# A gated graph network and an attention layer: gates r and z from seven block products, and LayerNorm's last pass on ScalarE

## The chip, the cores and the metric

The kernel runs on one core of a Trainium2 chip. Its time is the device time of one execution in microseconds (us). A core has a matrix engine (TensorE: PE for matmuls, PEld for the loads of their stationary operand), VectorE (DVE), ScalarE (ACT), GpSimd (POOL) and a queue engine (SP), each with an instruction stream of its own. Matmul results land in PSUM (8 banks of 512 fp32 columns on 128 partitions), which DVE and ACT read; everything else is held in SBUF.

## What is computed

64 graphs of 256 nodes with 256 features, an adjacency matrix for each. Layer 0 is a gated graph network with three rounds, layer 1 a graph attention with four heads; both take a normalised input and add to the residual stream.

```python
def _gru_cell(inp, h, w_ih, w_hh, b_ih, b_hh):
    gi = inp @ w_ih.T + b_ih
    gh = h @ w_hh.T + b_hh
    i_r, i_z, i_n = jnp.split(gi, 3, axis=-1)
    h_r, h_z, h_n = jnp.split(gh, 3, axis=-1)
    r = sigmoid(i_r + h_r); z = sigmoid(i_z + h_z)
    n = tanh(i_n + r * h_n)
    return (1.0 - z) * n + z * h

h = maximum(layernorm(x), 0)                      # layer 0
g = h
for i in range(3):
    m = einsum('bnd,de->bne', g, weight[i])
    g = _gru_cell(einsum('bst,bsd->btd', (adj != 0), m), g, w_ih, w_hh, b_ih, b_hh)
x = x + g
h = maximum(layernorm(x), 0)                      # layer 1
v = (h @ W.T + b) in 4 heads of 64
p = softmax over j of where(adj == 1, leaky_relu(l_src[i] + l_dst[j], 0.2), -9e15)
out = x + sum_j p[i, j] v[j]
```

## The kernel before

All arithmetic is fp32 (gather multiplies fp32r parts). Two graphs make a pair (32 pairs); a pair's 512 nodes are the 512 columns of a transposed tile `hT` with 256 features in two blocks of 128 partitions. At the start the message weights are multiplied into the input weights once, so a round is: `gather` (sum of the neighbours' states, exact adjacency times a state split into two parts `hi` and `lo`), then for each of two feature blocks four gates `hn`, `r`, `z`, `in` (line 288). A gate is one PSUM tile of 128 x 512 from the pool `ps_g` (four banks); r and z sum over four products (two blocks of `hT`, two of `aggr`), hn and in over two. A matmul in fp32 appears as two MATMUL instructions in the trace, called passes here. ACT and DVE then form r, z, n and the new state: tanh for the sigmoids (L302, L311), L303 and L306 for r times hn, L314 and L316 for n, a difference on POOL (L319), L320 and L323 for the state.

The order of work on PE is written by hand. `todo` holds pieces by slot and place; a slot has eight places, one gate each, and a slot is one round of one pair. Pair p has its rounds in slots 3p, 3p+2 and 3p+4, so that rounds of neighbouring pairs alternate and every slot is filled. The other pieces hang between the gates: `load` (SP), `prepare` (LayerNorm of x and the masks from adj), `turn` (transposes of the normalised rows), `split` (back to rows, hi and lo, from round 2 on), `gather`; for layer 1, `residual` (adds x, LayerNorm), `turn1`, `values`, `spread` (a row of scores through HBM to all partitions, `rows`), `score` (L375 to L387: masked scores, their maximum, exponentials and sums), `turn2`, `mix`, `finish`. The pattern repeats every three slots, one pair's whole work. Slots 1 (mod 3) hold two scores, slots 2 two more and the residual, slots 0 values and spread.

PE keeps the written order. On the other engines the order is made at build time from what is ready first in a planned time, earlier pieces first among those; on the chip each engine keeps that order and waits at the first instruction whose inputs are missing.

LayerNorm (`normalise`, L193) takes statistics per row on DVE (L198, L199), the power -1/2 on POOL (L202) and four DVE passes of 128 x 256 for (x - m) times the factor (L205). The ReLU follows where the rows are used: in the copy after the transposes (L215), in hi (L251) and lo (L252).

Of the kernel before, what the change touches and what calls it, by code (L numbers as in the profile page):

```python
# [17 lines left out]
P = 128  # L18
# [8 lines left out]
def gated_gnn_then_gat_kernel(  # L27
# [46 lines left out]
    ps_g = ctx.enter_context(tc.tile_pool(name="ps_g", bufs=4, space=bass.MemoryType.PSUM))  # L74
    ps_m = ctx.enter_context(tc.tile_pool(name="ps_m", bufs=4, space=bass.MemoryType.PSUM))

    def bank(name):
        return ps_m.tile([P, 512], F32, tag="mm", name=name)
# [6 lines left out]
    def load_first():  # L85
        xt = io.tile([P, R, D], F32, tag="x", name="x_0", bufs=4)
        nc.sync.dma_start(xt, x_rows[:T, :].rearrange("(r q) d -> q r d", q=P))
        at = io.tile([P, R, N], I32, tag="adj", name="adj_0", bufs=1)
        nc.sync.dma_start(at, adj_rows[:T, :].rearrange("(r q) t -> q r t", q=P))
        return xt, at  # L90
# [90 lines left out]

    setup_scope.close()
# [10 lines left out]
    def normalise(src, name):  # L193

        st = small.tile([P, R, 6], F32, tag="st", name=f"st_{name}")
        mv = small.tile([P, R, 2], F32, tag="mv", name=f"mv_{name}")
        for r in range(R):
            nc.vector.bn_stats(st[:, r, :], src[:, r, :])  # L198
            nc.vector.bn_aggr(mv[:, r, :], st[:, r, :])  # L199
        rstd = small.tile([P, R], F32, tag="rstd", name=f"rstd_{name}")  # L200
        nc.vector.tensor_scalar_add(rstd, mv[:, :, 1], EPS)
        nc.gpsimd.tensor_tensor(rstd, rstd, mhalf, ALU.pow)  # L202
        xn = sb.tile([P, R, D], F32, tag="xn", name=f"xn_{name}")
        for r in range(R):
            nc.vector.tensor_scalar(  # L205
                xn[:, r, :], src[:, r, :], mv[:, r, 0:1], rstd[:, r : r + 1], op0=ALU.subtract, op1=ALU.mult
            )
        return xn

    def relu_T(xn, dst, k, name):  # L210

        pt = bank(f"pt_{name}_{k}")
        for r in range(R):
            nc.tensor.transpose(pt[:, ts(r, P)], xn[:, r, ts(k, P)], ident)
        nc.scalar.activation(dst[:, k, :], pt, AF.Relu)  # L215

    def halves(name):
        hi = sb.tile([P, R, D], F32R, tag="hi", name=f"hi_{name}")
        lo = sb.tile([P, R, D], F32R, tag="lo", name=f"lo_{name}")
        return hi, lo  # L220

# [10 lines left out]
    class Pair:  # L232


        def __init__(self, p):
            self.p = p
            self.rden, self.pr, self.prT, self.oT = {}, {}, {}, {}

        def load(self):
            p = self.p  # L240
            self.xt = io.tile([P, R, D], F32, tag="x", name=f"x_{p}", bufs=4)
            nc.sync.dma_start(self.xt, x_rows[ts(p, T), :].rearrange("(r q) d -> q r d", q=P))
            self.at = io.tile([P, R, N], I32, tag="adj", name=f"adj_{p}", bufs=1)
            nc.sync.dma_start(self.at, adj_rows[ts(p, T), :].rearrange("(r q) t -> q r t", q=P))


        def prepare(self):
            p = self.p
            self.xn = normalise(self.xt, f"a{p}")
            self.hi, self.lo = halves(f"a{p}")  # L250
            nc.scalar.activation(flat(self.hi), flat(self.xn), AF.Relu)  # L251
            nc.vector.scalar_tensor_tensor(  # L252
                flat(self.lo), flat(self.xn), 0.0, flat(self.hi), op0=ALU.max, op1=ALU.subtract
            )
# [5 lines left out]
        def turn(self, k):  # L260
            if k == 0:
                self.hT = sb.tile([P, KD, T], F32, tag="hT", name=f"hT_{self.p}", bufs=5)
            relu_T(self.xn, self.hT, k, f"a{self.p}")

        def split(self, l):
            n_ = f"{self.p}_{l}"
            self.hi, self.lo = halves(n_)
            for i in range(PB):
                pt = natural(self.hT, i, n_)
                rows = batch_rows(i)  # L270
                nc.scalar.copy(flat(self.hi, rows), pt)
                nc.vector.tensor_sub(flat(self.lo, rows), pt, flat(self.hi, rows))

        def gather(self, l):
            n_ = f"{self.p}_{l}"
            self.aggr = sb.tile([P, KD, T], F32, tag="aggr", name=f"aggr_{n_}")
            for e in range(KD):
# [8 lines left out]
                nc.scalar.copy(self.aggr[:, e, :], pt)  # L286

        def gate(self, l, c, kind):

            n_ = f"{self.p}_{l}_{c}"  # L290
            hh, ih = wT["hh"], w_in[:, l]
            g = {"r": c, "z": KD + c, "hn": 2 * KD + c, "in": 2 * KD + c}[kind]
            pt = ps_g.tile([P, T], F32, tag="g", name=f"p{kind}_{n_}")
            parts = [(hh, self.hT, k) for k in range(KD)] if kind != "in" else []
            parts += [(ih, self.aggr, k) for k in range(KD)] if kind != "hn" else []
            for j, (w, src, k) in enumerate(parts):
                nc.tensor.matmul(pt, w[:, k, ts(g, P)], src[:, k, :], start=(j == 0), stop=(j == len(parts) - 1))  # L297
            if kind == "hn":
                self.p_hn = pt
            elif kind == "r":  # L300
                r_ = sb.tile([P, T], F32, tag="r", name=f"r_{n_}")
                nc.scalar.activation(r_, pt, AF.Tanh, bias=brz[:, g : g + 1], scale=0.5)  # L302
                nc.vector.tensor_scalar(r_, r_, 0.5, 0.5, op0=ALU.mult, op1=ALU.add)  # L303
                self.t_ = sb.tile([P, T], F32, tag="t", name=f"t_{n_}")
                g_n = 2 * KD + c
                nc.vector.scalar_tensor_tensor(  # L306
                    self.t_, self.p_hn, bh[:, g_n : g_n + 1], r_, op0=ALU.add, op1=ALU.mult
                )
            elif kind == "z":
                self.z_ = sb.tile([P, T], F32, tag="z", name=f"z_{n_}")  # L310
                nc.scalar.activation(self.z_, pt, AF.Tanh, bias=brz[:, g : g + 1], scale=0.5)  # L311
            else:
                t_, z_ = self.t_, self.z_
                nc.vector.tensor_add(t_, pt, t_)  # L314
                y_ = sb.tile([P, T], F32, tag="n", name=f"n_{n_}")
                nc.scalar.activation(y_, t_, AF.Tanh, bias=bi[:, g : g + 1])  # L316

                d_ = sb.tile([P, T], F32, tag="d", name=f"d_{n_}")
                nc.gpsimd.tensor_sub(d_, self.hT[:, c, :], y_)  # L319
                nc.vector.scalar_tensor_tensor(d_, z_, 1.0, d_, op0=ALU.add, op1=ALU.mult)  # L320
                if c == 0:
                    self.hT2 = sb.tile([P, KD, T], F32, tag="hT", name=f"hT_{self.p}_{l}", bufs=5)
                nc.vector.scalar_tensor_tensor(self.hT2[:, c, :], d_, 0.5, y_, op0=ALU.mult, op1=ALU.add)  # L323
                if c == KD - 1:
                    self.hT = self.hT2
# [11 lines left out]
        def turn1(self):  # L337
            self.hbT = sb.tile([P, KD, T], F32, tag="hbT", name=f"hbT_{self.p}", bufs=1)
            for k in range(KD):
                relu_T(self.xn, self.hbT, k, f"b{self.p}")  # L340
# [27 lines left out]
        def score(self, i, s):  # L368
# [4 lines left out]
            zz = sb.tile([P, H, N], F32, tag="zz", name=f"zz_{p}_{r}", bufs=3)  # L373
# [16 lines left out]
        def turn2(self, i, s):  # L390
# [3 lines left out]
            for j in range(KN):  # L394
# [4 lines left out]
                if j % 2:  # L399
                    nc.vector.tensor_copy(dst, src)  # L400
                else:
                    nc.scalar.copy(dst, src)

        def mix(self, i):
# [11 lines left out]
            self.oT[i] = sb.tile([P, H // 2, N], F32, tag="oT", name=f"oT_{p}_{i}")  # L416
            nc.scalar.copy(flat(self.oT[i]), po)

        def finish(self, i):
# [7 lines left out]
            o = sb.tile([P, KN, D], F32, tag="o", name=f"o_{p}_{i}")  # L427
# [13 lines left out]
    todo = {}  # L441

    def at(slot, k, piece, *args):
        todo.setdefault(8 * slot + k, []).append((piece, args))

    KINDS = ("hn", "r", "z", "in")
    pairs = [Pair(p) for p in range(NPAIR)]
    pairs[0].xt, pairs[0].at = first
    for q in pairs:
# [3 lines left out]
        at(s0 - 2, 2, q.prepare)  # L453
        at(s0 - 1, 2, q.turn, 0)
        at(s0 - 1, 3, q.turn, 1)
        at(s0 - 1, 6, q.gather, 0)
        for l in range(L):
            s = s0 + 2 * l
            if l:
                at(s - 1, 3, q.split, l)  # L460
                at(s - 1, 6, q.gather, l)
            for k in range(8):
                at(s, k, q.gate, l, k // 4, KINDS[k % 4])
        s += 1
        at(s, 4, q.residual)
        at(s + 1, 1, q.turn1)
        for r in range(R):
            at(s + 1, 3 + r // 2, q.values, r)
        at(s + 1, 6, q.spread)
        for piece, i, j, *place in (  # L470
            (q.score, 0, 0, 2, 1), (q.score, 0, 1, 2, 3), (q.turn2, 0, 0, 2, 6), (q.turn2, 0, 1, 3, 0),
            (q.score, 1, 0, 2, 6), (q.score, 1, 1, 3, 1), (q.turn2, 1, 0, 3, 6), (q.turn2, 1, 1, 4, 0),
        ):
            at(s + place[0], place[1], piece, i, j)
        at(s + 3, 2, q.mix, 0)
        at(s + 3, 4, q.finish, 0)
        at(s + 4, 2, q.mix, 1)
        at(s + 4, 6, q.finish, 1)

    for place in todo.values():  # L480
        place.sort(key=lambda x: x[0].__name__ == "gather")
    for place in todo.values():
        place.sort(key=lambda x: x[0].__name__ == "gate")
# [34 lines left out]
```

## Time and profile before

| | |
|---|---|
| runs, median | 2801.98 us (2799.52 to 2802.9, three) |
| profiled execution, its own time | 2799.7 us |
| its span, first to last instruction | 2797.7 us |
| mean granted TensorE clock | 0.993 |
| gate matmuls, passes of 128 x 512 | 6 groups of x768 |
| transposes, passes of 128 x 128 | x2560 in the steady part |
| gather, passes of 128 x 256 | x1536 |
| HBM traffic | 69.87 MB read, 17.04 MB written |

The span is cut into forty slices of 70 us. Busy tenths of an engine and the granted clock in each:

```profile
PE   7999999999999999999999999999999999999995
DVE  4346666556656556656566656566656566665466
ACT  1224434334433334343333443343443344443343
PEclk9999999999999999999999999999999999999998
```

Matmul records last to the end of their pipeline, so the durations of neighbours overlap; the distance from start to start is the pitch that counts. The costliest groups, with busy time and mean ns of one after the bar:

```profile
L297 PE MATMUL pz<-hT,hh_T 128*128 128x512 f32 x768 | 363.9, 596 | 0.0
L297 PE MATMUL pr<-aggr,w_in 128*128 128x512 f32 x768 | 360.9, 592 | 0.0
L302 ACT ACTIVATE r<-pr,brz 128x512 f32<-128x512 f32 x192 | 131.5, 685 | 526.5 <-PE pr L297 526.3
L379 DVE SCALAR_TENSOR_TENSOR zz<-zz 128x1024 f32<-128x1024 f32 x128 | 155.4, 1214 | 1.1
L400 DVE COPY prT<-ppT 128x512 f32<-128x512 f32 x128 | 87.0, 680 | 1.5 <-PE ppT L397 1.5
L351 DVE TENSOR_TENSOR val<-pv,b_val 128x264 f32<-128x264 f32 x128 | 52.3, 427 | 151.1 <-PE pv L348 151.1
L126 ACT COPY msgT<-pmT 128x256 f32<-128x256 f32 x6 | 1.9, 375 | 11.0 <-PE pmT L125 11.0
```

### The profile page before, as it was taken

Reading aid. Unit: us, or ns where it says so; the run is one execution under the profiler, and the core shown is the slowest. Engines: PE = TensorE matmul, PEld = TensorE weight load, DVE = VectorE, ACT = ScalarE, POOL = GpSimd, SP = SyncE. Lnnn points to the kernel's source line nnn. Section 1 sums busy time; section 2 is a strip of 40 time slices with the busy share of each in tenths; the row PEclk is TensorE's granted clock in tenths of the full one; section 3 lists DMA queues with packets and bytes.
Section 4 is the critical chain, followed back from the end, with each engine's and each line's share of the span. In section 5 each row is a group of like instructions: output and inputs, shape, how many; then the busy total and the mean of one; then the engine's idle time right before and its main releaser. Section 6 shows DMA issues by size and latency. Waiting matters only on the chain. (4 is left out here: it accounts for less than half of the span.)

```text
span 2797.7 us, 28381 instructions
## 1 busy us (share of the span) xinstructions
PE 2744.3 (98%) x10468; PEld 1518.7 (54%) x10468; DVE 1670.1 (60%) x3326; ACT 1053.5 (38%) x2311; POOL 413.6 (15%) x327
## 2 busy tenths in 40 slices
PE   7999999999999999999999999999999999999995
PEld 4455555555555555555555555555555555555553
DVE  4346666556656556656566656566656566665466
ACT  1224434334433334343333443343443344443343
POOL 0011111111111111111111111111111111111111
PEclk9999999999999999999999999999999999999998
DMA  3000110110110100101101101101101101100000
GB/s 92 8 31 12 38 38 27 38 38 12 39 31 34 38 26 24 38 27 38 38 16 34 38 27 38 38 12 38 38 27 39 38 12 38 38 27 23 23 23 31
DMA packets 61451, 88.73 MB, mean 32 GB/s; under 512 B 5248, under 2 KB 57088, under 8 KB 57216
## 3 DMA queue, kind: packets, MB, share of 16 engines
q1 hardware_dynamic: 56064, 84.16, 9.4%
q10 hardware_dynamic: 5248, 2.76, 0.4%
q8 instruction: 82, 1.34, 0.2%
q14 instruction: 57, 0.47, 0.1%
HBM read 69.87 MB, written 17.04 MB: 31 GB/s over the span
## 5 line engine op out<-in xcount | busy, mean ns | idle before, releaser
L319 POOL TENSOR_TENSOR d<-hT,n 128x512 f32<-128x512 f32 x192 | 265.5, 1383 | 1667.5 <-ACT n L316 1667.5
L384 ACT ACTIVATE zz<-zz,nmx 128x256 f32<-128x256 f32 x512 | 254.0, 497 | 292.3 <-DVE nmx L381 292.3
L297 PE MATMUL pz<-hT,hh_T 128*128 128x512 f32 x768 | 363.9, 596 | 0.0
L297 PE MATMUL phn<-hT,hh_T 128*128 128x512 f32 x768 | 362.7, 595 | 0.0
L297 PE MATMUL pin<-aggr,w_in 128*128 128x512 f32 x768 | 361.1, 593 | 0.0
L297 PE MATMUL pr<-hT,hh_T 128*128 128x512 f32 x768 | 361.0, 592 | 0.0
L297 PE MATMUL pz<-aggr,w_in 128*128 128x512 f32 x768 | 360.9, 592 | 0.0
L297 PE MATMUL pr<-aggr,w_in 128*128 128x512 f32 x768 | 360.9, 592 | 0.0
L302 ACT ACTIVATE r<-pr,brz 128x512 f32<-128x512 f32 x192 | 131.5, 685 | 526.5 <-PE pr L297 526.3
L314 DVE TENSOR_TENSOR t<-pin,t 128x512 f32<-128x512 f32 x192 | 131.4, 684 | 324.9 <-PE pin L297 324.8
L320 DVE SCALAR_TENSOR_TENSOR d<-z,d 128x512 f32<-128x512 f32 x192 | 132.6, 691 | 242.2 <-POOL d L319 242.2
L311 ACT ACTIVATE z<-pz,brz 128x512 f32<-128x512 f32 x192 | 130.7, 681 | 384.6 <-PE pz L297 384.6
L375 DVE SCALAR_TENSOR_TENSOR zz<-rows,val,noedge 128x256 f32<-128x256 f32 x512 | 220.9, 480 | 66.0 <-DMA rows<-line 66.0
L297 PEld LDWEIGHTS pz<-aggr,w_in 128*128 128x128 f32 x768 | 146.0, 190 | 183.6 <-issue 183.6
L297 PEld LDWEIGHTS pr<-aggr,w_in 128*128 128x128 f32 x768 | 146.0, 190 | 183.6 <-issue 178.6
L297 PEld LDWEIGHTS pr<-hT,hh_T 128*128 128x128 f32 x768 | 143.7, 190 | 169.3 <-issue 159.3
L297 PEld LDWEIGHTS pin<-aggr,w_in 128*128 128x128 f32 x768 | 138.7, 190 | 139.1 <-issue 137.0
L316 ACT ACTIVATE n<-t,bi 128x512 f32<-128x512 f32 x192 | 138.2, 720 | 187.7 <-DVE t L314 185.4
L297 PEld LDWEIGHTS phn<-hT,hh_T 128*128 128x128 f32 x768 | 139.6, 192 | 127.5 <-issue 121.7
L297 PEld LDWEIGHTS pz<-hT,hh_T 128*128 128x128 f32 x768 | 133.8, 190 | 120.8 <-issue 120.8
L397 PEld LDWEIGHTS ppT<-ident,zz 128*128 128x128 f32 x1024 | 120.8, 142 | 82.2 <-issue 57.8
L379 DVE SCALAR_TENSOR_TENSOR zz<-zz 128x1024 f32<-128x1024 f32 x128 | 155.4, 1214 | 1.1
(91 smaller groups left out, 3552.8 us busy)
## 6 DMA issues: line engine op xcount, KB each, us to landing
rows<-line SPq DMA_DIRECT2D x32, 1024.0 KB, 6.6
x<-in_x_dram SPq DMA_DIRECT2D x32, 512.0 KB, 4.0
adj<-in_adj_dram SPq DMA_DIRECT2D x32, 512.0 KB, 3.9
out_dram<-o SPq DMA_DIRECT2D x64, 256.0 KB, 2.2
w_msg<-in_L_gnn_weight_dram ACTq DMA_DIRECT2D x1, 768.0 KB
ih_nat<-in_L_gnn_w_ih_dram ACTq DMA_DIRECT2D x1, 768.0 KB
hh_nat<-in_L_gnn_w_hh_dram ACTq DMA_DIRECT2D x1, 768.0 KB
line<-srow SPq DMA_DIRECT2D x32, 8.0 KB
```

What stands on the lines that cost most here:

```text
L297: nc.tensor.matmul(pt, w[:, k, ts(g, P)], src[:, k, :], start=(j == 0), stop=(j == len(parts) - 1))
L302: nc.scalar.activation(r_, pt, AF.Tanh, bias=brz[:, g : g + 1], scale=0.5)
L311: nc.scalar.activation(self.z_, pt, AF.Tanh, bias=brz[:, g : g + 1], scale=0.5)
L314: nc.vector.tensor_add(t_, pt, t_)
L316: nc.scalar.activation(y_, t_, AF.Tanh, bias=bi[:, g : g + 1])
L319: nc.gpsimd.tensor_sub(d_, self.hT[:, c, :], y_)
L320: nc.vector.scalar_tensor_tensor(d_, z_, 1.0, d_, op0=ALU.add, op1=ALU.mult)
L375: nc.vector.scalar_tensor_tensor(zz[:, h, :], self.rows[:, h, ts(i, N)], self.val[:, r, D + h : D + h + 1], self.noedge[:, r, :], op0=ALU. ...
L379: nc.vector.scalar_tensor_tensor(flat(zz), flat(zz), ALPHA, flat(zz), op0=ALU.mult, op1=ALU.max)
L384: nc.scalar.activation(zz[:, h, :], zz[:, h, :], AF.Exp, bias=nmx[:, h : h + 1], accum_out=den[:, h : h + 1])
L397: nc.tensor.transpose(pt[:, ts(h, P)], self.pr[r][:, h, ts(j, P)], ident)
```

## The change

For r and for z the product is a 2 x 2 block matrix (output blocks and feature blocks of 128) times a 2 x 2 block matrix (feature blocks, and the pair's two graphs of 256 columns). Eight block products become seven, from sums of blocks: of the weights, made once at the start (`block_sums`), and of the columns, made in each round (`column_sums`, for hT on POOL, for aggr on DVE). The sums over hh and in run in the same PSUM columns. Two banks serve a gate: half of `px` takes products 1, 6, 7 and 4 one after the other, and is copied out between them (`ab`, `c22`); `pyz` takes 5 and 3 in one half and 2 in the other. hn and in keep their 512 columns, now issued one matmul at a time between the products. A slot has 22 units (`U`). The two PSUM pools of four banks become one of eight.

In LayerNorm ACT makes ReLU(x * rstd - m * rstd) in one pass per row block (`shift` is -m * rstd); the later copies lose their ReLU, round 1's hi and lo move to the slot of `split`. The copies of `prT` all go to ACT. The buffers of x, xn, hi, lo, hT, zz, oT and o shrink, and the places are rewritten in units.

```diff
-    ps_g = ctx.enter_context(tc.tile_pool(name="ps_g", bufs=4, space=bass.MemoryType.PSUM))
-    ps_m = ctx.enter_context(tc.tile_pool(name="ps_m", bufs=4, space=bass.MemoryType.PSUM))
+    ps = ctx.enter_context(tc.tile_pool(name="ps", bufs=8, space=bass.MemoryType.PSUM))
...
+    def block_sums(w, name):
+        out_ = const.tile([P, 4, 2, P], F32, name=f"sums_{name}")
...
+        nc.vector.tensor_add(out_[:, 0], a21, a22)
+        nc.vector.tensor_sub(out_[:, 1], out_[:, 0], a11)
+        nc.vector.tensor_sub(out_[:, 2], a11, a21)
+        nc.vector.tensor_sub(out_[:, 3], a12, out_[:, 1])
+        return out_
...
-            nc.vector.tensor_scalar(
-                xn[:, r, :], src[:, r, :], mv[:, r, 0:1], rstd[:, r : r + 1], op0=ALU.subtract, op1=ALU.mult
+            nc.scalar.activation(
+                xn[:, r, :], src[:, r, :], AF.Relu, bias=shift[:, r : r + 1], scale=rstd[:, r : r + 1]
             )
...
+    def column_sums(src, engine, name):
+        t = sb.tile([P, 4, N], F32, tag=f"sum{name[0]}", name=f"sum_{name}")
+        s_ = src.rearrange("q k (i n) -> q k i n", i=PB)
+        engine.tensor_sub(t[:, 0::2, :], s_[:, :, 1, :], s_[:, 0, :, :])
+        engine.tensor_add(t[:, 1, :], t[:, 2, :], s_[:, 0, 0, :])
+        engine.tensor_sub(t[:, 3, :], s_[:, 1, 0, :], t[:, 1, :])
+        return t
...
+            if l == 0:
+                nc.scalar.copy(flat(self.hi), flat(self.xn))
+                nc.vector.tensor_sub(flat(self.lo), flat(self.xn), flat(self.hi))
+                return
...
+        def product(self, l, kind, m):
...
+            x_, y_, z_ = self.px[:, :N], self.pyz[:, :N], self.pyz[:, N:]
+            out_ = {1: x_, 6: x_, 7: x_, 4: x_, 5: z_, 3: z_, 2: y_}[m]
+            parts = ((wT["hh"], sums_h, self.hT, self.th), (w_in[:, l], sums_in[l], self.aggr, self.ts_))
...
+                nc.tensor.matmul(
+                    out_, lhs, rhs, start=(j == 0 and m in (1, 5, 2)), stop=(j == 1), skip_group_check=True
+                )
...
+            if m == 1:
+                nc.scalar.copy(self.ab[:, 0, :], x_)
+            elif m == 6:
+                nc.scalar.copy(self.ab[:, 1, :], x_)
+            elif m == 5:
+                nc.scalar.copy(self.c22, z_)
+            elif m == 7:
+                nc.vector.tensor_add(self.c22, x_, self.c22)
+                tanh(self.g_[:, 3, :], self.c22, 1)
+            elif m == 2:
+                nc.vector.tensor_add(flat(self.ab), self.pyz, flat(self.ab))
+                tanh(flat(self.g_[:, :2, :]), flat(self.ab), 0)
+                if kind == "r":
+                    self.reset(l, 0)
+            elif m == 4:
+                tanh(self.g_[:, 2, :], x_, 1)
+                if kind == "r":
+                    self.reset(l, 1)
...
-                if j % 2:
-                    nc.vector.tensor_copy(dst, src)
-                else:
-                    nc.scalar.copy(dst, src)
+                nc.scalar.copy(dst, src)
...
+    UNITS = [
+        *("r1 r5 hn00 r6 hn01 r3 hn10 r7 hn11 r2 r4".split()),
+        *("z1 z5 in00 z6 in01 z3 z7 in10 z2 in11 z4".split()),
+    ]
...
+        at(s0 - 2, 5, q.prepare)
+        at(s0 - 1, 5, q.turn, 0)
+        at(s0 - 1, 8, q.turn, 1)
         for l in range(L):
             s = s0 + 2 * l
...
+            at(s - 1, 9, q.split, l)
+            at(s - 1, 10, q.sum_h)
+            at(s - 1, 17, q.gather, l)
...
+            at(s, 20, q.update, l, 0)
+            at(s, 21, q.update, l, 1)
         s += 1
+        at(s, 12, q.residual)
+        at(s + 1, 3, q.turn1)
...
+        at(s + 1, 17, q.spread)
...
+            (q.score, 0, 0, 2, 3), (q.score, 0, 1, 2, 8), (q.turn2, 0, 0, 2, 17), (q.turn2, 0, 1, 3, 0),
+            (q.score, 1, 0, 3, 0), (q.score, 1, 1, 3, 4), (q.turn2, 1, 0, 3, 17), (q.turn2, 1, 1, 4, 0),
```

## The prediction

> **What bounds the kernel now.** First the page's busy times, then the stretches of one steady period, then TensorE's timeline.
>
> ```profile
> PE 2744.3 (98%) x10468; PEld 1518.7 (54%) x10468; DVE 1670.1 (60%) x3326; ACT 1053.5 (38%) x2311; POOL 413.6 (15%) x327
> ```
>
> ```profile
> 90.00:1385.00 1295.00, 1295.00 (x4909) 713.23 (x4908) 770.12 (x1531) 491.71 (x1059) 194.45 (x151) 1.00 0.09 30
> 1385.00:1411.00 26.00, 26.00 (x85) 13.40 (x84) 20.30 (x36) 11.49 (x30) 3.25 (x2) 1.00 0.15 54
> 1411.00:1440.00 29.00, 29.00 (x122) 16.20 (x121) 18.77 (x48) 11.69 (x28) 5.79 (x5) 1.00 0.09 28
> 1440.00:1471.00 31.00, 31.00 (x125) 17.82 (x124) 12.56 (x21) 10.23 (x16) 3.88 (x3) 1.00 0.12 31
> ```
>
> The columns are length, then busy time of PE, PEld, DVE, ACT and POOL. From 90 us on PE is never idle, at the full granted clock. The last three rows are one period of three slots, one pair's work: 86.0 us, 32 of them. DVE is busy 51.6 of the 86 us, but 20.3 of 26 in the first slot. So PE bounds; what follows needs the pitch of its instructions, because its durations overlap.
>
> ```profile
> 1450.20 1.88 PE L297 MATMUL pz<-aggr,w_in 128*128 128x512 f32 x4
> 1451.92 1.94 PE L348 MATMUL pv<-w_val,hbT 128*128 128x264 f32 x8
> 1453.70 1.04 PE L227 MATMUL pn<-ident,hT 128*128 128x128 f32 x8
> ```
>
> Four passes over 512 columns start 1.72 us before what follows them: 430 ns a pass (each fp32 matmul is two passes). Eight passes over 264 columns take 1.78 us: 222.5 ns, or 0.843 ns a column, against 0.840 for 512. A pass of 256 columns should then cost 215 to 222 ns; I take 216. At 264 columns every pass has its own weights too, so a new weight load per narrow pass is already covered by this row.
>
> **The gain.** In each of the 96 slots r and z now take 16 matmuls = 32 wide passes, 32 x 0.430 = 13.76 us. After: 2 gates x 7 products x 2 sources x 2 passes = 56 passes x 0.216 = 12.10 us. Saved 1.66 us a slot, 159 us in all; at 222.5 ns a pass it is 1.30 us and 125 us. hn, in, gather and the transposes keep their passes. I take 158.
>
> [...]
>
> **What the other engines pay, per period.** DVE gains three column sums a slot (one 512 wide like L323, 0.69, two 256 wide like L351's 0.43), two c22 additions (0.43) and two 512-wide additions into ab (0.69): 3.8 us a slot, 11.4; shift 0.3. It loses 8 L205 (0.41 each, 3.3) and 4 L400 (0.68, 2.7). Net +5.7: 57 of about 81 us. ACT gains 18 copies of 256 columns (375 ns in L126, at most L384's 497: I take 0.375, 6.8 us), six tanh more, since each gate's two of 512 columns (0.685, L302) become one and two halves (0.45 each, between 0.375 and 0.5; 1.3), 8 passes of xn (0.4 each, 3.2) and 4 prT copies (0.58, 2.3): +13.6, so 47 of 81. POOL gains three sums a slot: L319's 1.27 us for 512 wide, and 0.64 to 1.27 for each narrow one (I take 0.65): 2.6 a slot, 7.8. None of the three becomes the bound by its sum. Sixteen block sums at the start (0.41 each, 6.6 us of DVE) lie in gaps DVE has while it waits for L131; 2 us are charged for what sticks out and 1 for the tail's prT copies, now on one engine.
>
> Edits I cost at nothing: fewer buffers (x, xn, hi, lo, zz, hT, o, oT). xn has one buffer: prepare's copy is last read by split at unit 9 of slot 2 (mod 3), residual's is written some 6 us after unit 12 and first read at unit 3 of the next slot, thirteen units and 11 us on; if that cover went, PE would wait there for the rest. hi and lo are read by gather eight units after they are written and rewritten a slot later. The x load, issued on SP ahead of adj, now waits for the residual one slot before; it lands in 4.0 us and its first use is over a slot later. If that wait came late by some us on SP, line, rows and out behind it would slip; rows is the one that matters, at 2 us a period.
>
> **Where a stall comes from.** Now a gate's bank is read once, at the end, and four banks rotate. After the change px is written, copied, and added to again, and half of pyz too, so PE waits for ACT or DVE inside a gate. Per slot: r1 to r6, z1 to z6 and z6 to z7 (ACT), and r7 to r4 (DVE), each with two units of 0.86 us = 1.72 between; r5 to r3, r6 to r7, z5 to z3 (ACT) and z7 to z4 (DVE) with three, 2.58. A return trip with a free engine takes the pipeline's end (1.88 - 1.72 = 0.16), a copy (0.375, or 0.43 on DVE) and two signals (0.04 to 0.2): about 0.7. The spare is 1.0 or 1.9 us. Everything behind a waiting matmul on PE waits with it. How promptly are PE's results read today?
>
> ```profile
> 1407.59 1.88 PE L297 MATMUL pz<-aggr,w_in 128*128 128x512 f32 x4
> ```
>
> ```profile
> 1410.11 0.51 ACT L384 ACTIVATE zz<-zz,nmx 128x256 f32<-128x256 f32 x1 [3.45 <-DVE nmx L381]
> ...
> 1412.10 0.67 ACT L311 ACTIVATE z<-pz,brz 128x512 f32<-128x512 f32 x1
> ```
>
> pz is ready at 1409.47. ACT is idle but stands at an exponential that waits for DVE's maximum, then runs four: z starts 2.63 us late. A pin ready at 1411.19 is read by L314 at 1414.63, 3.4 us late, behind scores. Nothing waits for either today. Which waits recur:
>
> ```profile
> ACT zz L384 <- DVE nmx L381: 292.3, 127, 11.0
> DVE d L320 <- POOL d L319: 242.2, 163, 2.2
> DVE zz L375 <- DMA rows<-line: 66.0, 29, 6.6
> ```
>
> ACT stands 2.3 us at each of 4 score rows a period and then is busy 2.0 more. With ACT returns every 4.5 us on average, about one a burst is caught, in a random part of it: a loss of 0 to 1.6 us (2.6 less the spare of 1.0), I take 0.4, as about half the returns have the longer spare. Four give 1.6. In the score slot rows come 2.3 us late (66.0 / 29), which moves the row's ten DVE and ACT instructions and the c22 addition of r7 queued among them: 2.3 less 1.0 is 1.3 at most, 0 at least; I take 0.8. Together 2.4 us a period, 77 us.
>
> POOL's sums lengthen this if they meet DVE:
>
> ```profile
> 1404.04 1.98 POOL L319 TENSOR_TENSOR d<-hT,n 128x512 f32<-128x512 f32 x1 [14.23 <-ACT n L316]
> ```
>
> Alone it takes 1.27; here it starts during L379 (both DVE inputs in SBUF) and ends 0.71 later. [...] DVE has 24 us a period free, so the sum above leaves it out and the range's top has it.
>
> **The sum.** Against the profiled execution: 2799.7 - 158 + 3 + 77 = 2721.7. It stands 2.3 us below the median of 2801.98, inside its runs. I forecast 2722.
>
> **Rivals.** (1) Every return comes in time, PE stays gapless: 2799.7 - 158 + 3 = 2645, at most 2665 with 0.6 us a period. For it: DVE and ACT are under 75% by their sums, and the order on DVE is filled greedily (the xn_a of 1438.9 is for transposes one period after those of 1419.0, 66 us later). Against: the two late reads above lie in an ordinary period. Chance 0.20.
> (2) Slower: returns coupled to the score rows. Each of the 4 bursts catches a return with the short spare (1.6 each, 6.4), and r7 to r4 waits out rows and a POOL meeting (1.3 + 1.3), less the 2 that one stall spares the next: 7 us a period, 224 us: 2869. It decides above (158 - 3) / 32 = 4.8 us a period. For it: DVE busy 20.3 of 26 us in that slot, +3.8 less a third of what leaves it, 2.0, in a slot PE now crosses in some 24; the banks px, pyz and in or hn then fill up too. Against: stalls give DVE and ACT time to catch up, and the slot at 12.56 of 31 us absorbs a lag. With a middling 5 to 6 us the time is 2805 to 2840. Chance 0.24.
> (3) The narrow passes don't give the saving: at 222.5 ns it is 125 us and with the same stalls 2755; it is nil at 246 ns. Against: the 264-column row. Chance 0.06.
> (4) The forecast, some stalls, 1 to 4.4 us a period: 2675 to 2785. Chance 0.50.
>
> The range is 2650 to 2830: about 0.1 is left below, in case 1, and 0.1 above, in case 2. The forecast's own range is 2675 to 2785. Runs of this kernel tell 0.2% (5.6 us) from no change. Faster: 0.20 + 0.48 of case 4 + 0.03 of case 3 = 0.71; within 0.2%: 0.04; slower: 0.25.
>
> **What would show it.** Pass pitch: groups of px and pyz matmuls at 0.86 us a unit where nothing waits; over 0.9 refutes the gain. Stalls: idle time of PE or PEld ahead of the second writes of px and pyz, put down to ACT's ab or c22 copies or DVE's c22 addition, 40 to 130 us in sum, most of it in the slots with scores; if it is under 20, case 1, if over 155, case 2. Idle time ahead of other products, put down to the column sums (r5, z5), would be a wait I have costed at nothing: after gather, six units lie before r5's second half, 5 us against 2.3. A DVE busy time far from 1855 us, ACT from 1490 or POOL from 665 would refute the rows used.

## The result, and the profile after

The changed kernel takes 2872.52 us (median of 4 runs, 2870.39 to 2875.74) beside 2802.23 for the kernel before: ratio 1.0254, 95% interval 1.0236 to 1.0271. It is 70 us slower, and the profiled execution (2872.8) is 228 us above the 2645 that the prediction gave for a TensorE without gaps.

Busy times on the page of the changed kernel, then its own stretches over one period (length; busy time of PE, PEld, DVE, ACT, POOL; granted clock):

```profile
PE 2644.2 (92%) x12772; PEld 1957.0 (68%) x12772; DVE 2022.2 (70%) x3694; ACT 1449.6 (50%) x3463; POOL 695.7 (24%) x615
```

```profile
1407.00:1438.00 31.00, 26.99 (x124) 20.01 (x123) 23.30 (x39) 15.02 (x39) 8.47 (x7) 0.94 0.17 60
1438.00:1467.00 29.00, 29.00 (x152) 21.81 (x151) 23.90 (x46) 15.00 (x39) 8.23 (x7) 1.00 0.09 28
1467.00:1494.30 27.30, 26.04 (x125) 19.09 (x124) 14.93 (x33) 15.09 (x33) 5.00 (x5) 1.00 0.01 2
```

PE, which was never idle in the steady part, now is for 5.3 of 87.3 us, 4.0 of them in the first stretch, and there the clock falls to 0.94. No other engine is a bound by its sum. The waits of PE, with their total, number and longest:

```profile
PE px_z L355 <- ACT ab_z L364: 73.1, 30, 2.5
PE px_r L355 <- DVE c_r L370: 46.4, 30, 1.8
PE px_z L355 <- DVE c_z L370: 36.9, 28, 2.3
...
PE px_r L355 <- ACT ab_r L364: 14.6, 20, 1.7
```

These are z1 to z6, r7 to r4, z7 to z4 and r1 to r6: four returns inside a gate, 171 us. The first three come once in nearly every period, at the same place, and each of these three has its own cause in the timeline (start, duration, engine, instruction; in brackets the idle time before it and what ended it).

**r7 to r4, in the slot with the first two scores.**

```profile
1417.93 4.02 DVE L464 SCALAR_TENSOR_TENSOR zz<-rows,val,noedge 128x256 f32<-128x256 f32 x5
...
1424.54 0.41 DVE L370 TENSOR_TENSOR c_r<-px_r,c_r 128x256 f32<-128x256 f32 x1
...
1418.16 1.38 POOL L244 TENSOR_TENSOR sum_h<-hT 128x512 f32<-128x512 f32 x1 [1.60 <-DVE hT L412]
1419.62 0.79 POOL L245 TENSOR_TENSOR sum_h<-sum_h,hT 128x256 f32<-128x256 f32 x1
1420.48 0.79 POOL L246 TENSOR_TENSOR sum_h<-hT,sum_h 128x256 f32<-128x256 f32 x1
...
1420.38 0.59 PE L355 MATMUL px_r<-sum_s,sums_in 128*128 128x256 f32 x2
1420.81 1.02 PE L397 MATMUL phn<-hT,hh_T 128*128 128x512 f32 x2
...
1422.98 0.59 PE L355 MATMUL pyz_r<-aggr,w_in 128*128 128x256 f32 x2
1425.09 0.67 PE L355 MATMUL px_r<-sum_h,hh_T 128*128 128x256 f32 x2 [1.52 <-DVE c_r L370]
```

The two passes at 1420.38 cross in 0.43 us, two of 512 columns in 0.86: the narrow pass costs 0.215 us where nothing waits. r7 is done at 1420.97, but DVE adds it to c22 only at 1424.54, behind the scores. Five score instructions, each with both inputs in SBUF, take 4.02 us; where no sums ran on POOL (e2 below) the same five take 2.06. They run beside POOL's three sums, from 1418.16 to 1421.27. r4 starts 1.68 us late.

**z1 to z6, in the same slot.**

```profile
1424.65 0.51 ACT L473 ACTIVATE zz<-zz,nmx 128x256 f32<-128x256 f32 x1 [6.71 <-DVE nmx L470]
...
1428.95 0.50 ACT L473 ACTIVATE zz<-zz,nmx 128x256 f32<-128x256 f32 x1
...
1430.92 0.35 ACT L364 COPY ab_z<-px_z 128x256 f32<-128x256 f32 x1
...
1427.76 1.08 PE L397 MATMUL pin<-aggr,w_in 128*128 128x512 f32 x2
1431.33 0.70 PE L355 MATMUL px_z<-sum_h,sums_h 128*128 128x256 f32 x2 [2.49 <-ACT ab_z L364]
...
1432.29 1.57 PE L397 MATMUL pin<-aggr,w_in 128*128 128x512 f32 x2
1433.66 1.06 PE L355 MATMUL pyz_z<-hT,sums_h 128*128 128x256 f32 x2
1434.51 1.06 PE L355 MATMUL pyz_z<-aggr,sums_in 128*128 128x256 f32 x2
```

ACT stood 6.71 us for a maximum, then made two bursts of four exponentials with the r gate's tanh and hi between. z1 ended near 1427.05; its copy stands behind the second burst and starts 3.9 us after. PE stops for 2.49 us, and 1.3 us after it resumes its clock halves (from 1432.63 for 3.41 us): the pair of wide passes at 1432.29 takes 1.37 us instead of 0.86, the narrow pair at 1433.66 takes 0.85 instead of 0.43. In the stretch from 1434 to 1438 the granted clock is 0.74.

**z7 to z4, in the slot with the residual.**

```profile
1465.47 1.23 DVE L219 SCALAR_TENSOR_TENSOR shift_b<-mv_b,rstd_b 128x4 f32<-128x4 f32 x1 [1.13 <-POOL rstd_b L217]
...
1469.68 0.16 DVE L219 SCALAR_TENSOR_TENSOR shift_a<-mv_a,rstd_a 128x4 f32<-128x4 f32 x1 [1.12 <-POOL rstd_a L217]
1469.76 0.42 DVE L370 TENSOR_TENSOR c_z<-px_z,c_z 128x256 f32<-128x256 f32 x1
...
1465.41 1.27 POOL L405 TENSOR_TENSOR t<-hT,n 128x512 f32<-128x512 f32 x1
...
1470.24 0.70 PE L355 MATMUL px_z<-sum_h,hh_T 128*128 128x256 f32 x2 [1.26 <-DVE c_z L370]
```

The four-column product for `shift` takes 1.23 us beside POOL's difference and 0.16 alone, and twice DVE stands more than a microsecond for POOL's power. The addition of z7 waits behind all that.

Counted as starts later than the usual pitch, from 700 to 2200 us, these three cost 2.65 (z6), 1.70 (r4) and 1.49 us (z4) a period and r6 some 0.5; the rest of about 8 is passes at half clock and small gaps.

The groups that grew (busy, mean ns of one; idle before, split by releaser):

```profile
L464 DVE SCALAR_TENSOR_TENSOR zz<-rows,val,noedge 128x256 f32<-128x256 f32 x512 | 297.6, 625 | 52.4 <-PE ppT L486 42.5 <-DMA rows<-line 9.9
L412 DVE SCALAR_TENSOR_TENSOR hT<-t,n 128x512 f32<-128x512 f32 x192 | 169.3, 882 | 6.5
L219 DVE SCALAR_TENSOR_TENSOR shift_b<-mv_b,rstd_b 128x4 f32<-128x4 f32 x32 | 38.1, 1191 | 36.2 <-POOL rstd_b L217 36.2
```

Before, the hT instruction had a mean of 686 ns (L323) and a score's mean was 480. The two grew through different POOL instructions: without POOL's sums (e1 below) a score is back at 515 ns, but hT stays at 882. Half of the 192 hT instructions overlap one of POOL's differences t (L405), and these have a mean of 1075 ns; the other half have 689. The time by which a DVE instruction is longer beside POOL is counted as busy: 512 scores at 625 ns in place of e1's 515 are 57 us of DVE's 2022, and 96 hT at 1075 in place of 689 are 37. Rows, which DVE waited 66 us for before, now come 9.9 us late in the whole run.

### The profile page after: what moved, and what is told of

Same layout as the page of the kernel before. It is cut to its first block, busy times and chain, and to the rows that moved or that the text cites. A ratio compares the mean times of both kernels' runs of the same rounds, so it can differ in the third digit from the quotient of the medians.

```text
span 2871.0 us, 35051 instructions
## 1 busy us (share of the span) xinstructions
PE 2644.2 (92%) x12772; PEld 1957.0 (68%) x12772; DVE 2022.2 (70%) x3694; ACT 1449.6 (50%) x3463; POOL 695.7 (24%) x615
## 5 line engine op out<-in xcount | busy, mean ns | idle before, releaser
L405 POOL TENSOR_TENSOR t<-hT,n 128x512 f32<-128x512 f32 x192 | 278.3, 1450 | 1445.2 <-ACT n L403 1445.2
L244 POOL TENSOR_TENSOR sum_h<-hT 128x512 f32<-128x512 f32 x96 | 125.5, 1307 | 424.1 <-ACT hT L232 306.2
L312 PE MATMUL pa<-edge,hi 128*128 128x256 f32 x768 | 198.6, 296 | 0.2 <-ACT hi L292 0.2
L312 PE MATMUL pa<-edge,lo 128*128 128x256 f32 x768 | 190.4, 285 | 0.8 <-DVE lo L293 0.7
L409 DVE SCALAR_TENSOR_TENSOR t<-g_z,t 128x512 f32<-128x512 f32 x192 | 132.0, 688 | 76.6 <-POOL t L405 71.8
L355 PE MATMUL px_z<-sum_h,sums_h 128*128 128x256 f32 x384 | 118.0, 388 | 73.1 <-ACT ab_z L364 73.1
L412 DVE SCALAR_TENSOR_TENSOR hT<-t,n 128x512 f32<-128x512 f32 x192 | 169.3, 882 | 6.5
L486 PE MATMUL ppT<-ident,zz 128*128 128x128 f32 x1024 | 141.3, 280 | 18.6 <-ACT zz L473 18.5
L470 DVE TENSOR_REDUCE nmx<-zz 128x4 f32<-128x1024 f32 x128 | 154.8, 1210 | 0.1
L312 PEld LDWEIGHTS pa<-edge,lo 128*128 128x128 f32 x768 | 148.7, 194 | 1.5 <-DVE lo L293 1.0
L312 PEld LDWEIGHTS pa<-edge,hi 128*128 128x128 f32 x768 | 148.3, 193 | 1.6 <-ACT hi L292 0.6
```

Of the source, the lines that this page charges most:

```text
L312: nc.tensor.matmul(pt[:, ts(i, N)], y[:, r, ts(e, P)], self.edge[:, r, :], start=(j == 0), stop=(j == len(parts) - 1),)
L405: nc.gpsimd.tensor_sub(t_, self.hT[:, c, :], y_)
L412: nc.vector.scalar_tensor_tensor(self.hT2[:, c, :], d_, 0.5, self.y_[c], op0=ALU.mult, op1=ALU.add)
L470: nc.vector.tensor_reduce(nmx, zz, AX.X, ALU.max, negate=True)
L486: nc.tensor.transpose(pt[:, ts(h, P)], self.pr[r][:, h, ts(j, P)], ident)
```

## The experiments

The theory was that PE stops at four returns whose answers are late through POOL meeting DVE and through ACT's order; the rivals were DVE's amount of work and LayerNorm's move to ACT. All ratios are to the kernel before.

**e1: no column sums of hT.**

```diff
-            at(s - 1, 10, q.sum_h)
...
-            parts = ((wT["hh"], sums_h, self.hT, self.th), ...
+            parts = ((wT["hh"], sums_h, self.hT, None), ...
+                def col(n):
+                    return b(n % 2, n // 2) if cols is None else cols[:, n]
```

> Leaves out the column sums of hT that POOL makes (288 of POOL's instructions); the products take plain blocks of hT in their place, so r and z are other numbers. Theory A (the loss is four waits inside the gates, and POOL's sums cause the largest by blocking DVE's score instructions: five of them took 4.0 us where five alone take 2.1): the wait of r4 for DVE's c22 addition falls from 1.7 us a period to under 0.5, that of z6 for ACT's copy from 2.65 to under 1.5, and the time falls by 60 to 110 us, to 2762 to 2812. Theory B (DVE and ACT simply have too much work in the score slots, ports don't matter): DVE and ACT lose no instruction, so the time stays at 2872 within 15.

Measured 2801.65 us, 1.0002 (0.9992 to 1.0013). Its waits of PE:

```profile
PE px_z L358 <- ACT ab_z L367: 70.4, 30, 2.5
...
PE px_z L358 <- DVE c_z L373: 8.3, 28, 1.2
...
PE px_r L358 <- DVE c_r L373: 0.8, 2, 0.5
```

The r4 wait falls from 46.4 to 0.8 us and z4's from 36.9 to 8.3, together 74 us, beside a gain of 71. So POOL's sums make the r4 wait, and z4's wait is small without them. The z6 wait stays whole, against theory A: it has another cause.

**e2: the same sums on DVE.**

```diff
-            self.th = column_sums(self.hT, nc.gpsimd, f"h_{self.p}")
+            self.th = column_sums(self.hT, nc.vector, f"h_{self.p}")
```

> The same sums on DVE in place of POOL: 1.5 us more DVE work a slot, 4.6 a period, and no meeting between them. Theory A (the meeting costs, not the amount): the score instructions return to 0.48 us each, the r4 wait shrinks, time 2800 to 2860. Theory B (amount of work): DVE goes from 61 to 65 us a period, the waits grow, time 2880 to 2960.

Measured 2782.16 us, 0.9933 (0.9918 to 0.9948): 90 us less than the change, though DVE has 288 instructions more. The five scores, and ACT's order in that slot:

```profile
1379.36 2.06 DVE L464 SCALAR_TENSOR_TENSOR zz<-rows,val,noedge 128x256 f32<-128x256 f32 x5
...
1388.42 0.36 ACT L364 COPY ab_z<-px_z 128x256 f32<-128x256 f32 x1
1388.67 0.51 ACT L473 ACTIVATE zz<-zz,nmx 128x256 f32<-128x256 f32 x1
```

```profile
PE px_z L355 <- DVE c_z L370: 42.8, 28, 1.7
...
PE px_z L355 <- ACT ab_z L364: 8.9, 28, 0.3
PE px_r L355 <- DVE c_r L370: 8.2, 28, 0.6
```

Two things changed at once: the meeting is gone (r4's wait falls from 46.4 to 8.2), and the order made at build time came out otherwise, with ab_z ahead of the second burst (z6's falls from 73.1 to 8.9). The amount of DVE's work alone is refuted as the cause. z4 is left, now behind a DVE that makes the sums itself.

**e12: e2, and `shift` made on POOL.** DVE negates the mean before POOL's power, POOL multiplies after it.

```diff
-        nc.gpsimd.tensor_tensor(rstd, rstd, mhalf, ALU.pow)
         shift = small.tile([P, R], F32, tag="shift", name=f"shift_{name}")
-        nc.vector.scalar_tensor_tensor(shift, mv[:, :, 0], -1.0, rstd, op0=ALU.mult, op1=ALU.mult)
+        nc.vector.tensor_scalar_mul(shift, mv[:, :, 0], -1.0)
+        nc.gpsimd.tensor_tensor(rstd, rstd, mhalf, ALU.pow)
+        nc.gpsimd.tensor_tensor(shift, shift, rstd, ALU.mult)
```

> The changed kernel's own order of units, with hT's sums on DVE and shift on POOL: two edits away from the change. With the sums on DVE z4 still waited 1.7 us a period for a c22 addition that stood behind shift_b (1.13 us waiting for POOL's power, 1.22 long for meeting POOL) and shift_a (1.12). Theory A: that wait goes to under 0.4, 2782 less 40: 2735 to 2755. Theory B (work only): 2775 to 2790.

Measured 2743.57 us, 0.9790 (0.9776 to 0.9805), 39 less than e2, against a c_z wait of 42.8 that falls to 0.2:

```profile
PE px_z L356 <- DVE c_z L371: 0.2, 1, 0.2
```

On POOL:

```profile
1400.93 1.02 POOL L219 TENSOR_TENSOR rstd_b<-rstd_b,mhalf 128x4 f32<-128x4 f32 x1 [3.58 <-DVE shift_b L218]
1402.03 0.20 POOL L220 TENSOR_TENSOR shift_b<-shift_b,rstd_b 128x4 f32<-128x4 f32 x1
```

The product costs POOL 0.20 us, and DVE's `shift` instruction no longer waits for the power. In e1 the stands and the long `shift` were as in the change (1.13, 1.25 and 1.12 us) and z4 still hardly waited, so that wait needs both: a DVE made late by the sums, and `shift` ahead of the addition. Two edits of a few lines take 129 us off the change.

**e10: the second score of that slot four units later.**

```diff
-            (q.score, 0, 0, 2, 3), (q.score, 0, 1, 2, 8),
+            (q.score, 0, 0, 2, 3), (q.score, 0, 1, 2, 12),
```

> One number of the changed kernel: the second score row of a slot is placed at unit 12 in place of 8, behind z1 (unit 11). Theory A2 (z6's wait of 2.65 us comes from ACT's order: two bursts of four exponentials stand ahead of the copy of z1): the copy now goes ahead of the second burst, z6's wait falls under 0.8 us, the half-clock intervals that followed it go too; time 2785 to 2815. Rival (the wait comes from DVE being late as a whole): z6's wait stays over 1.8 us, 2860 to 2885.

Measured 2812.90 us, 1.0041 (1.0027 to 1.0055):

```profile
PE px_r L355 <- ACT ab_r L364: 50.4, 31, 1.8
...
PE px_z L355 <- ACT ab_z L364: 14.7, 28, 0.5
```

With the burst moved the z6 wait falls by 58 us, so it was ACT's order. Now two exponentials of the following score row stand ahead of another return, r6, whose wait grows by 36. The stretches of half clock are gone: the granted clock from 90 to 2700 us is 1.00, against 0.99 in the change.

**e3: the products of r and z interleaved**, so that four or five units lie between the writes of one px (each gate's tiles kept apart in a dict).

```diff
-        *("r1 r5 hn00 r6 hn01 r3 hn10 r7 hn11 r2 r4".split()),
-        *("z1 z5 in00 z6 in01 z3 z7 in10 z2 in11 z4".split()),
+        *("r1 z1 r5 z5 hn00 r6 z6 hn01 r3 z3 hn10".split()),
+        *("r7 z7 hn11 r2 z2 r4 z4 in00 in01 in10 in11".split()),
```

> Only the order of the units changes: r1 z1 r5 z5 hn00 r6 z6 hn01 r3 z3 hn10 r7 z7 hn11 r2 z2 r4 z4 in00 in01 in10 in11. Each write into a bank that was read inside the gate now comes four or five units (3.4 to 4.3 us) after the write before it, not two or three. Theory A (answers are late by up to 3.9 us, seldom more; the spare of 1.0 or 1.9 us is what is too small): with 2.7 or more to spare the four waits fall from 6.4 to under 2 us a period, time 2660 to 2740. Theory B (queues are overloaded): the waits move to other places (in, next slot's first products) and the time stays above 2830. A third outcome, banks run out because six are held at once: new waits of products for free banks, over 2872.

Measured 2779.30 us, 0.9922 (0.9907 to 0.9937), between the ranges of theories A and B. The waits on ab are all but gone (1.0 us); r4 still waits for c_r (58.5 us in 30 waits, up to 2.2), since POOL's sums are still there, and layer 1's transposes of the residual now wait for a bank (20.9 us).

**e6: e3 and e2 together; e7: with `shift` on POOL too.**

> The interleaved units with hT's column sums on DVE, so both single edits together. In the interleaved run r4 still waited 2.1 us a period for a c22 addition behind score instructions that POOL's sums had blocked, and the clock was halved in 11 intervals of 3.4 us. Theory A: the 2.1 us and the half-clock intervals go, 2779 less 67 less 19: 2690, between 2665 and 2725. Theory B (the amount of work; the two edits removed the same waits): 2755 to 2785.

> As the run before in this list, with shift made on POOL behind the power, so that DVE doesn't stand at it (70 us of idle time in the changed kernel, and 1.19 us for shift_b against 0.16 for shift_a, a meeting with POOL). If that standing reaches PE: 10 to 30 us under the run before; if the wider spare already covers it: the same within 6.

Measured 2787.70 (0.9948, 0.9933 to 0.9962) and 2783.69 us (0.9936, 0.9921 to 0.9951). The gains don't add; e6 is 8 us above e3 alone and 63 above the upper end of its theory A. Its largest wait in sum, beside 28.1 us that r4 still waits for c_r:

```profile
PE pn_b L254 <- DVE o L516: 56.0, 30, 1.9
```

A new wait took the old one's place: r and z together hold four of the eight banks and hn or in two more, and the transposes of pn_b wait until finish has emptied one. The stretches of half clock, 11 in e3, are 21 in e6, each behind this wait: 17 us more (granted clock of the whole run 0.983 in e3, 0.978 in e6). In e7 the bank wait is 56.0 us again, and the time is 4 us under e6, so `shift` had next to nothing to give there.

**e11: e7, with r4 and z4 two units later and finish, residual and turn1 moved.**

```diff
-        *("r7 z7 hn11 r2 z2 r4 z4 in00 in01 in10 in11".split()),
+        *("r7 z7 hn11 r2 z2 in00 in01 r4 z4 in10 in11".split()),
...
-        at(s, 12, q.residual)
-        at(s + 1, 3, q.turn1)
+        at(s, 18, q.residual)
+        at(s + 1, 6, q.turn1)
...
-        at(s + 3, 12, q.finish, 0)
+        at(s + 3, 9, q.finish, 0)
```

> The interleaved units with hT's sums on DVE and shift on POOL, and places mended where the run with both edits waited: r4 and z4 two units later (behind in00 and in01), finish(0) at unit 9 and residual at 18 (they waited 1.9 us for a bank there, six being held by the interleaved gates), turn1 at unit 6. Theory A (each wait is one answer that comes too late or one bank too few, and the half-clock intervals only follow waits of about 2.5 us): waits under 1.5 us a period, no half-clock intervals, 2660 to 2715. Theory B (DVE and ACT are overloaded in the two score slots, waits only move): over 2745.

Measured 2708.36 us (2705.14 to 2709.86), 0.9663 (0.9647 to 0.9679): the fastest, ahead of both kernels.

```profile
PE ppT L489 <- DVE ab_r L376: 30.6, 30, 1.2
```

No return inside a gate is among its large waits; one bank wait of a microsecond a period is. Several pieces moved at once, and which of them gave how much wasn't tried.

**e4 and e5: LayerNorm alone.** e4 is the kernel before with the last pass, ReLU and `shift` as in the change; e5 the change with the old pass on DVE.

```diff
-            nc.vector.tensor_scalar(
-                xn[:, r, :], src[:, r, :], mv[:, r, 0:1], rstd[:, r : r + 1], op0=ALU.subtract, op1=ALU.mult
+            nc.scalar.activation(
+                xn[:, r, :], src[:, r, :], AF.Relu, bias=shift[:, r : r + 1], scale=rstd[:, r : r + 1]
             )
...
```

> The kernel before with LayerNorm's last pass on ACT alone, gates untouched. Nothing on PE depends on it within several us, so all theories expect 2802 within 6; a change beyond that would give the LayerNorm move a price of its own, and then the seven products' share is smaller.

> The changed kernel with LayerNorm's last pass put back on DVE (four passes of 128 x 256 for each norm, the ReLU again in the later copies). It is the other half of the change undone alone. Theory A (waits inside the gates): the r4 and z6 waits lie in the slot without a norm and stay; the z4 wait may go up or down, as DVE stands for POOL's power either way; 2840 to 2900. Theory C (the LayerNorm move is what costs, DVE standing at shift): under 2820.

e4 2802.82 us, 1.0004 (0.9994 to 1.0013); e5 2888.00 us, 1.0304 (1.0289 to 1.032). Where PE waits for nobody the move changes nothing; in the change it is worth 15 us. In e5 z4 waits 41.6 us and r4 48.9 (36.9 and 46.4 in the change), and there are 20 stretches of half clock instead of 15, at 1.7 us each (clock of the whole run 0.980, against 0.984): together 16 us. LayerNorm's move is not the cause of the loss.

## Why the prediction was wrong

**The gain held.** A narrow pass was put at 216 ns (bounds 215 and 222); it takes 215.5 to 216. From one `prow` transpose to its like a pair later is 84.4 us before, and 87.2 after (mean of the 28 steady periods) with about 8 of lost time in it: some 79 without, a saving in the size of the predicted 5.0 a period. e11 shows that it can be had: 94 us below the kernel before. The start and the tail (3 us) were not measured apart.

**The stall term failed**: "Together 2.4 us a period, 77 us". It is 7.1 (228 / 32) over the whole run. Rival (2), at 7 us a period and 2869, gave the time, but that its number fits so well is luck. It had four bursts at 1.6 each, rows at 1.3 and a POOL meeting at 1.3, less 2. What came is one pair of bursts at 2.65, the meeting at 1.70, a z4 wait of 1.49 behind `shift`, some 0.5 on r6, and half clock. Point by point:

- *Four bursts at 0.4 each, as if returns fell at random into them.* They don't. The order of every engine is fixed at build time, so a return meets the same burst in each period or in none: z6 lost 2.65 us in 17 of 17 periods. Two bursts ahead of one copy were not looked for, and 2.65 is above even the 1.6 of the upper end. e10 and e2 show it from both sides.
- *Rows late in the score slot, 0.8 on r7 to r4.* The place was right, the cause wrong: rows are late by 9.9 us in the run, not 66. The scores ahead of the addition were late through POOL's sums.
- *POOL's meeting left out of the sum*, because "DVE has 24 us a period free". That free time is an average; what counts is the 1.0 us of spare between r7 and r4 when the meeting falls there. No run shows the 1.3 us that rival (2) has for a meeting; r4 waited 1.70 us a period, and e1, without the sums, is 71 us faster. Three pairs were seen to meet, and DVE's instruction was longer in each: five scores beside sum_h 4.02 us (2.06 in e2, where no sums run on POOL), hT beside t 1075 ns in the mean (689 where they don't overlap), `shift` beside t 1.23 us (0.16 alone).
- *`shift` at 0.3 us a period.* It costs 1.19 + 0.16 us and two stands of 1.1 us at POOL's power, which the text did not price. e12 shows 39 us for it, with the sums on DVE.
- *The clock.* The sum had no term for it. Stretches of 3.4 us at half clock, which the kernel before has none of in its steady part, appear 15 times: each costs 1.7 us, 26 us in all.
- *The sum of these*: 171 us of waits inside gates, some 0.16 us more at each of 108 for the pipeline's end (17), and 26 for the clock make 214 of 228. The other 14 are not traced.

**Busy times**: ACT 1450 (1490 predicted) and POOL 696 (665) are near, though xn takes 0.59 to 0.60 us and not 0.4; DVE 2022 (1855) holds the blocked time. The period of 86.0 us, read from three hand-cut stretches, is 84.4; no term of the sum used it. No recurring wait of PE is put down to the buffers costed at nothing.

## What to carry to other kernels

Before a result that nobody waits for becomes one that the bottleneck reads back, list for each return its spare and the instructions that stand ahead of the answering one in that engine's order; free time on average says nothing. An order that is fixed at build time makes a late answer late in every period, so price it whole or at nothing, and move it by putting the instruction elsewhere. After each stall that is removed, look for the next holder: e6 gave its gain to the banks.

## What the runs showed of the hardware

A four-column DVE product of two SBUF tiles took 1.23 us beside POOL's 512-column difference and 0.16 alone: what is blocked need not be large.

A wait of PE of 1.9 us was enough for a 3.4-us stretch at half clock, though not in every period. The change has 15 in its steady part, behind waits of 2.3 to 2.5 us; e6 has 21, all behind the bank wait, at 1.90 to 1.92 (30 such waits in its run, 56.0 us); e2 and e10, whose recurring waits end at 1.7 and 1.8, have none (both have a granted clock of 1.00 from 90 to 2700 us), though e1 has one behind a wait of 1.71 (at 2580 us).

What picks the periods can be read from the starts of the stretches. In the change all 20, those at its two ends included, lie within 5 ns of a grid of 3.413 us that runs through the whole execution: 1258.55, 1432.63 and 1695.46 us, for instance, are 51 and 77 steps apart. Of its 29 steady waits of 2.3 us and more, the 15 that had 2.03 us or more inside one interval of the grid were each followed by a stretch; the other 14, which the grid divides so that neither part is over 1.93, were not. So in these 29, all but one of 2.49 us, where a wait falls on the grid decided. Near 1.9 us this gives no sharp limit: a part of 1.93 us (at 2040.20) was followed by no stretch in the change, and the waits of 1.90 to 1.92 in e6 by 21.
